# Two transformer layers on one core: earlier inputs, mask parts made on the chip, normalization and key halves on GpSimd, and another order of the projections

## The chip, the cores and the metric

The kernel runs on one core of one Trainium2 chip. The metric is the device time in microseconds, the median of the runs. A core has five engines that run side by side, each with its own queue in program order: TensorE (PE; its weight loads are shown as PEld), VectorE (DVE), ScalarE (ACT), GpSimd (POOL) and SyncE (SP), which here only issues DMAs. PE writes its results into PSUM banks; a bank comes free again once another engine has read it.

## The reference

x has 4 sequences of 2048 tokens and 256 channels. Four sublayers follow each other, each on a layer-normalized x and each added to x:

```python
x = x + _L0_attn_ref(_layernorm(x, axis=-1), ...)   # 1 head of 64, causal, biases
x = x + _L0_ffn_ref(_layernorm(x, axis=-1), ...)    # clip to fp8 e4m3, one 256x256 product, bias
x = x + _L1_attn_ref(_layernorm(x, axis=-1), ...)   # 16 heads of 16, rotary, causal
x = x + _L1_ffn_ref(_layernorm(x, axis=-1), ...)    # mix with the token before; sigmoid(r) * (relu(k)^2 Wv)
```

Everything but the fp8 product is computed in float32. `_layernorm` subtracts the mean and divides by the root of the variance plus 1e-5.

## The kernel before

**Tiling.** A block is 512 tokens of one sequence (`BLK`), four tiles of 128 (`TT`); a sequence has 4 blocks (`qb` 0 to 3), so there are 16 blocks, in the order of `order`. Because of the causal mask, block `qb` attends to `qb + 1` blocks of keys. Many helpers work on a half block (`hf`), two tiles.

**Stages of a block**, each a Python generator that emits instructions and yields a rough cost:
- first layer (list `A`): `a_in` normalizes, transposes and projects; `a_mid` computes row maxima, scores, exponentials and the weighted values; `a_out` does the output product, the next normalization to fp8 (`q8`, then float16 `q16`), the FFN product and the sum into x.
- second attention, preparation (lists `Bq` and `Q`): `b_in` normalizes and transposes; `b_project` makes q, k, v for each tile and rotates q and k with five GpSimd operations; `b_keys` splits the keys into an upper half in another float32 form (`F32R`) and a lower half, the difference, and transposes them; `b_queries` copies, transposes and splits the queries.
- second attention, main loop: 4 groups of 4 heads (`g`, NG = 4), and in a group `TT * (qb + 1)` steps (`kt`), one for each tile of keys. A step emits `scores` (L622, mask at L632), four exponentials on ScalarE (L644), the weighted values of the step before (`weighted`, L651), and, by `run_maxima`, the maxima of the group after (`maxima`, L597, mask at L605, reduction on VectorE at L610).
- end (list `E`): `end_half` does the output product, normalizes, mixes tokens (`mix`, ScalarE and VectorE), and computes the last FFN and the store.

**What sets the order.** The instructions of each of PE, ACT, DVE and POOL run in the order in which Python emitted them (a last loop ties each to the one before). The main loop adds a credit `rate_of(...)` in each step and `pull` spends it on the generators of E, Bq, Q and A, each of which advances at most once in a step where it yields a cost of zero or more. So work of the next block and of the block before is laid between the steps of the current one. `rate_of` spreads the remaining cost of each list over the steps until it is due: A and Bq by the third group, E and Q by the fourth. What isn't done by then is emitted at once by `force`: Bq before the maxima of the next block begin, in the last group of the current one; E and Q at the block's end.

**The start.** Constants first: identities and masks on GpSimd, then DMAs in SyncE's queue: the first block's x, weights, and 48 small copies (L187) that place 32-row pieces of an identity and two masks (`ident_p`, `mask_p`, `maskT_p`, used by L605 and L632) on every group of 32 partitions. VectorE prepares the fp8-clipped FFN weight (L155 to L161) and two small constants. Then the first two blocks are prepared in a loop of their own: block 0 up to its queries, block 1 (`A2`) beside it while the credit stays above a floor. The second block's x is loaded by `a_of(1)`, which stands after the copies in the program.

`normalize` (L241) is called by `normal_T` (for `a_in`, `b_in` and `end_half`) and by `a_out`; `stats` before it computes mean and variance on VectorE (L229, L230) and the power of -0.5 on GpSimd (L232, L234). The lower half of the keys is at L528, the copy of the transposed fp8 tile at L449, the edge copies that `mix` needs at L699 and L701, the sums of x on GpSimd at L437, L458 and L742, the rotation at L496 to L505, and the copy of queries at L558.

Of the kernel before, what the change touches and what calls it, by code (L numbers as in the profile page):

```python
# [22 lines left out]
P = 128  # L23
C = 256
# [18 lines left out]
def seq_kernel(  # L43
# [63 lines left out]
    def load_x(b, qb):  # L107
# [14 lines left out]
    bf_bc = load_row(bf, "bf_bc", C)  # L122


    wo0 = const.tile([D0 + 1, C + 1], F32, name="wo0")
# [12 lines left out]
    nc.vector.tensor_scalar(omu_sb, mu_sb, -1.0, 1.0, ALU.mult, ALU.add)  # L138
    cos_sb = const.tile([P, T // P, DK // 2], F32, name="cos_sb")
    nc.sync.dma_start(cos_sb, cosd)  # L140
    sin_sb = const.tile([P, T // P, DK // 2], F32, name="sin_sb")
    nc.sync.dma_start(sin_sb, sind)
    nsin_sb = const.tile([P, T // P, DK // 2], F32, name="nsin_sb")
    nc.vector.tensor_scalar_mul(nsin_sb, sin_sb, -1.0)

    wf16 = const.tile([P, CK, C], F16, name="wf16")
    wcf, wce, wcm = (
        work.tile([P, CK * C], F32, tag="w2", name=f"wc{i}", bufs=W2) for i in range(3)  # L150
    )
    nc.sync.dma_start(
        wcf.rearrange("p (k n) -> p k n", k=CK), wfT.rearrange("(k p) n -> p k n", p=P)
    )
    nc.vector.tensor_scalar(wcf, wcf, 448.0, -448.0, ALU.min, ALU.max)  # L155
    nc.vector.tensor_scalar(
        wce.bitcast(I32), wcf.bitcast(I32), 0x7F800000, None, ALU.bitwise_and
    )
    nc.vector.tensor_scalar(wcm, wce, 2.0**-6, 1.5 * 2.0**20, ALU.max, ALU.mult)
    nc.vector.tensor_tensor(wcf, wcf, wcm, ALU.add)  # L160
    nc.vector.tensor_tensor(  # L161
        wf16.rearrange("p k n -> p (k n)"), wcf, wcm, ALU.subtract
    )

# [13 lines left out]


    parts = []
    for src, name in ((ident_b, "ident_p"), (mask_b, "mask_p"), (maskT_b, "maskT_p")):
        t = const.tile([P, HG, P], BF16, name=name)
        for h in range(HG):
            for v in range(HG):
                nc.sync.dma_start(  # L187
                    t[h * SLOT : (h + 1) * SLOT, v, :], src[v * SLOT : (v + 1) * SLOT, :]
                )
        parts.append(t)  # L190
    ident_p, mask_p, maskT_p = parts

# [26 lines left out]
    def full(n, keep=2):  # L219
        return live[0] + n > W2 - keep  # L220
# [13 lines left out]
        nc.gpsimd.tensor_tensor(y, v, mhalf[:, :2], ALU.pow)  # L234
        return mv, y

    def normalize(x, hf, my, dst):

        mv, y = my
        for j in range(2):  # L240
            nc.vector.tensor_scalar(  # L241
                dst[:, j, :], x[:, 2 * hf + j, :], mv[:, j, 0:1], y[:, j : j + 1],
                ALU.subtract, ALU.mult, saturate=False,
            )
# [18 lines left out]
    def normal_T(x, out_to, hf, tag):  # L263

        my = stats(x, hf, tag)
        yield 0.0
        while full(2):
            yield None
        xn = w2n(f"xn_{tag}_{hf}")
        normalize(x, hf, my, xn)  # L270
        yield 0.0
        if not out_to:
            out_to.append(w2t(f"xT_{tag}_{hf}"))
        transpose(xn, out_to[0], f"{tag}_{hf}", nc.scalar.copy)
        done(1)
        yield 0.6
# [134 lines left out]
    def a_out(b, qb, x, hf):  # L411

        tag = f"a0_{b}_{qb}"
        while (b, qb) not in ctx0:
            yield None
        cx = ctx0[b, qb]
        t2 = slice(2 * hf, 2 * hf + 2)
        for t in range(2 * hf, 2 * hf + 2):
            o = bank(f"po_{tag}_{t}")
            nc.tensor.matmul(  # L420
                o[:, : C + 1], cx[:, t * P : (t + 1) * P], wo0, start=True, stop=True
            )
            rs = small.tile([P, 1], F32, tag="rs0", name=f"rs_{tag}_{t}")
            nc.vector.reciprocal(rs, o[:, C : C + 1])
            nc.vector.scalar_tensor_tensor(
                x[:, t, :], o[:, :C], rs, x[:, t, :], ALU.mult, ALU.add
            )
        if hf:
            done(1)
        my = stats(x, hf, f"f{tag}")  # L430
        yield 1.0

        q8 = work.tile([P, 2, C], FP8, tag="q8", name=f"q8_{tag}_{hf}", bufs=2)
        normalize(x, hf, my, q8)
        q16 = work.tile([P, 2, C], F16, tag="h16", name=f"q16_{tag}_{hf}", bufs=3)
        nc.gpsimd.tensor_copy(q16, q8)
        nc.gpsimd.tensor_tensor(  # L437
            x[:, t2, :], x[:, t2, :], bf_bc[:, None, :].to_broadcast([P, 2, C]), ALU.add
        )
        yield 0.0  # L440
        pt = bank(f"ptf_{tag}_{hf}", F16)
        for k in range(CK):
            for j in range(2):
                at = k * HALF + j * P
                nc.tensor.transpose(
                    pt[:, at : at + P], q16[:, j, k * P : (k + 1) * P], ident_h
                )
        qhT = work.tile([P, CK, HALF], F16, tag="h16", name=f"qhT_{tag}_{hf}", bufs=3)
        nc.vector.tensor_copy(qhT, pt[:, :BLK].rearrange("p (k n) -> p k n", k=CK))  # L449
        yield 0.5  # L450
        po = bank(f"pof_{tag}_{hf}")
# [66 lines left out]
    def b_keys(b, qb):  # L518

        tag = f"a1_{b}_{qb}"  # L520
        for t in range(TT):
            while (b, qb, t) not in roped or count[0] < roped[b, qb, t][0] + 2:
                yield None
            _, qk, kn = roped.pop((b, qb, t))
            kn2 = kn.rearrange("p (h z d) -> p h z d", z=2, d=DK)
            rk = qk[:, C:].rearrange("p (h d) -> p h d", d=DK)
            nc.scalar.copy(kn2[:, :, 0, :], rk)
            nc.vector.tensor_tensor(  # L528
                kn2[:, :, 1, :], rk, kn2[:, :, 0, :].bitcast(F32), ALU.subtract
            )  # L530
# [12 lines left out]
            done(1)  # L543
            flags.add((b, qb, "k", t))
            yield -0.5
# [130 lines left out]
    def end_half(b, qb, x, cn, hf):  # L676
# [22 lines left out]
            nc.gpsimd.tensor_copy(xs_[:, :, 0:1], edges.pop((b, qb - (1 - hf), 1 - hf)))  # L699
        edges[b, qb, hf] = small.tile([P, CK, 1], F32, tag="edge", name=f"edge_{tag}", bufs=3)  # L700
        nc.gpsimd.tensor_copy(edges[b, qb, hf], xs_[:, :, HALF : HALF + 1])  # L701
        while full(3) or (hf and (b, qb, "mid") not in flags):
            yield None
        mix = []
# [81 lines left out]

    def a_of(i):
        b, qb = order[i]
        if i > 0:
            xs[b, qb] = load_x(b, qb)  # L790
        x = xs[b, qb]
        a_load[0] += 13 + 9 * (qb + 1)
        return [a_out(b, qb, x, 0), a_out(b, qb, x, 1), a_mid(b, qb),
                a_in(b, qb, x, 0), a_in(b, qb, x, 1)]
# [73 lines left out]
    def rate_of(i, g, kt, n):  # L868

        to = lambda where: max(where * n - (g * n + kt), 1)  # L870
        rate = BASE
        first = a_load[0] if a_next == i + 2 else 0.0
        if first > 0 or Bq:
            rate = max(rate, first / to(1.5), (first + b_load[0] + e_load[0] / 2) / to(3))
        return max(rate, (q_load[0] + e_load[0]) / to(4))


    A.extend(a_of(0))
# [28 lines left out]
    for G, (i, b, qb, g) in enumerate(groups):  # L907
# [5 lines left out]
        for kt in range(n):  # L913
# [122 lines left out]
```

## Time and profile before

| | |
|---|---|
| runs, median (lowest to highest) | 3472.14 us (3472.14 to 3476.44), 3 runs |
| profiled execution, its own time | 3472.42 us |
| its span | 3470.6 us |
| mean granted PE clock | 0.928 |
| PE / DVE / ACT / POOL busy | 3179.8 / 2045.0 / 1801.8 / 634.7 us |
| L241 on DVE, 128x256: for `xn_a`, `q_a`, `xn_f` | x128, x64, x64: 48.6, 31.6, 30.0 us |
| L528 on DVE, 128x256 | x64, 33.9 us |
| L449 on DVE, 128x512 | x32, 12.3 us |
| L558 on POOL, copy of 128x256 | x128, 407 ns each |
| L505 on POOL, two inputs of 128x256 | x64, 730 ns each |
| L187 on SP, mask copies | x48 |

The span runs from the first instruction to the last on the core; the run's own time is a little longer. Busy time is the sum of an engine's instructions without overlap. A row of the timeline has start, time, engine, line, operation, output and inputs, shapes and count; in brackets stands how long the engine was idle before it and whose result ended that. A row of a table by stretches has, for each engine, busy us and (in brackets) the number of instructions, then the mean clock that PE was granted (1.00 is full), the share of time in which DMA engines were busy and what they moved in GB/s.

### The profile page before, as it was taken

To read this page: it belongs to the slowest core of one execution; us is meant where nothing else is said; L and a number is where in the kernel's file an instruction comes from. 1 tells how busy PE (TensorE), PEld (TensorE's weight loads), DVE (VectorE), ACT (ScalarE), POOL (GpSimd) and SP (SyncE) were. 2 spreads that over 40 slices of the span, in tenths; PEclk is the share of its full clock that TensorE was granted. 3 is DMA by queue.
4 is the path that set the end of the run, shared out by engine and by line. 5 is a ranking of instruction groups with operands and counts; after the bars stand their busy time and mean duration, and the time that the engine had idled before them with its cause. 6 is when DMAs were issued, how large, how long until landed. Compare 5 with 4: busy or idle time off the path is not lost.

```text
span 3470.6 us, 75157 instructions
## 1 busy us (share of the span) xinstructions
PE 3179.8 (92%) x31392; PEld 1736.6 (50%) x31392; DVE 2045.0 (59%) x4439; ACT 1801.8 (52%) x3678; POOL 634.7 (18%) x985
## 2 busy tenths in 40 slices
PE   3799999999998999999999899899999899989998
PEld 2455545454455554545446454444545555444444
DVE  2465656666645675576645665567663567555662
ACT  1345446455554644646555464555655454554555
POOL 1421303121112300313003220122110321021000
PEclk9899899989997999989999799998999899998899
DMA  2000000000000000000000000000000000000000
GB/s 61 1 2 14 1 2 14 1 4 10 1 2 13 14 2 1 13 1 14 2 1 8 7 14 2 4 10 1 14 2 2 13 5 5 1 7 1 7 2 7
DMA packets 22918, 24.78 MB, mean 7 GB/s; under 512 B 3953, under 2 KB 22322, under 8 KB 22578
## 3 DMA queue, kind: packets, MB, share of 16 engines
q1 hardware_dynamic: 22578, 19.97, 1.8%
q8 instruction: 247, 4.05, 0.5%
q14 instruction: 93, 0.76, 0.1%
HBM read 11.18 MB, written 8.39 MB: 6 GB/s over the span
## 4 chain that ended last, share of the span: by engine, by line
PE 71%; DVE 17%; ACT 5%; POOL 3%; issue 3%; SPq 1%; DMA 0%; POOLq 0%; ACTq 0%; DVEq 0%
PE s L622 16%; PE av L651 15%; PE m L597 11%; DVE mx L610 11%; PE av_a L398 3%; PE pq_a L258 3%; ACT p L644 2%; PE pv_a L258 2%; PE pk_f L721 2%; PE po_f L258 2%; PE s_a L386 1%; PE pw_f L258 1%; PE s L632 1%; PE pq_a L318 1%; PE pt_c L662 1%
## 5 line engine op out<-in xcount | busy, mean ns | idle before, releaser
L610 DVE TENSOR_REDUCE mx<-m 128x1 f32<-128x512 f32 (+3 forms) x2560 | 1378.8, 603 | 935.2 <-PE m L597 535.5
L644 ACT ACTIVATE p<-s 128x512 f32<-128x512 f32 (+3 forms) x2560 | 1206.2, 533 | 1009.2 <-PE s L622 517.0
L651 PE MATMUL av<-p,v_a 128*32 128x512 f32 (+3 forms) x5120 | 640.7, 572 | 0.0
L622 PE MATMUL s<-qh_a,kT_a 32*128 32x512 f32 (+3 forms) x2560 | 539.2, 475 | 60.8 <-DVE mx L610 30.2
L597 PE MATMUL m<-kT_a,qh_a 32*128 32x512 f32 (+3 forms) x2560 | 465.4, 488 | 60.2 <-ACT p L644 28.2
L597 PEld LDWEIGHTS m<-kT_a,qh_a 32*128 32x128 f32 x2560 | 207.8, 194 | 573.6 <-issue 154.0
L622 PEld LDWEIGHTS s<-qh_a,kT_a 32*128 32x128 f32 x2560 | 244.3, 189 | 412.7 <-DVE mx L610 120.4
L622 PE MATMUL s<-ql_a,kT_a 32*128 32x512 f32 (+3 forms) x2560 | 338.0, 407 | 0.0
L597 PE MATMUL m<-kT_a,ql_a 32*128 32x512 f32 (+3 forms) x2560 | 328.8, 410 | 0.0
L622 PE MATMUL s<-sh,ones 32*128 32x512 f32 (+3 forms) x2560 | 310.5, 378 | 0.0
L622 PEld LDWEIGHTS s<-sh,ones 32*128 32x128 f32 x2560 | 184.1, 194 | 18.8 <-ACT sh L292 1.6
L232 POOL TENSOR_SCALAR v_f<-mv_f 128x2 f32<-128x2 f32 x32 | 7.2, 225 | 1012.9 <-DVE mv_f L230 1012.4
L651 PEld LDWEIGHTS av<-p,v_a 128*32 128x32 f32 x5120 | 105.5, 111 | 166.4 <-issue 144.3
L597 PEld LDWEIGHTS m<-kT_a,ql_a 32*128 32x128 f32 x2560 | 163.4, 200 | 0.0
L622 PEld LDWEIGHTS s<-ql_a,kT_a 32*128 32x128 f32 x2560 | 160.8, 193 | 0.0
L398 PE MATMUL av_a<-p_a,v_a 128*65 128x512 f32 (+3 forms) x320 | 146.1, 538 | 0.5
L394 ACT ACTIVATE p_a<-s_a 128x512 f32<-128x512 f32 (+3 forms) x160 | 85.4, 534 | 100.3 <-PE s_a L389 62.4
L258 PE MATMUL pq_a<-wqkv,xT_a 128*128 128x512 f32 x256 | 124.8, 610 | 0.9 <-ACT p L644 0.9
L232 POOL TENSOR_SCALAR v_a<-mv_a 128x2 f32<-128x2 f32 x64 | 14.1, 221 | 515.2 <-DVE mv_a L230 514.3
L605 PE MATMUL m<-mask_p,ident_p 32*128 32x128 bf16 (+3 forms) x4096 | 107.3, 205 | 0.0
L632 PE MATMUL s<-maskT_p,ident_p 32*128 32x96 bf16 (+3 forms) x4096 | 105.9, 199 | 0.0
L361 DVE TENSOR_REDUCE mx_a<-m_a 128x1 f32<-128x512 f32 (+3 forms) x160 | 87.7, 603 | 17.0 <-PE m_a L360 14.0
(156 smaller groups left out, 3913.8 us busy)
## 6 DMA issues: line engine op xcount, KB each, us to landing
x<-in_x SPq DMA_DIRECT2D x16, 512.0 KB, 4.0
out_y<-x SPq DMA_DIRECT2D x32, 256.0 KB, 2.1
wqkv<-in_wqkv1T SPq DMA_DIRECT2D x1, 768.0 KB, 8.7
wqk<-in_wqk0T SPq DMA_DIRECT2D x1, 256.0 KB, 4.4
wo<-in_wo1T SPq DMA_DIRECT2D x1, 256.0 KB, 9.1
wr<-in_wrT SPq DMA_DIRECT2D x1, 256.0 KB, 9.1
wk<-in_wkT SPq DMA_DIRECT2D x1, 256.0 KB, 7.2
wv<-in_wvT SPq DMA_DIRECT2D x1, 256.0 KB, 5.8
```

The lines of the kernel that those rows point to most:

```text
L258: nc.tensor.matmul(dst, lhsT[:, k, t * P : (t + 1) * P], w[:, k, :], start=(k == 0), stop=(k == CK - 1),)
L361: nc.vector.reduce_max(mx[:, t, kb : kb + 1], sc[:, :w], axis=AX.X)
L394: nc.scalar.activation(pT[:, c0:], sc[:, c0:], AF.Exp, scale=D0**-0.5)
L398: nc.tensor.matmul(av[: D0 + 1, c:], v0[k // TT][:, k % TT, :], p[:, c:], start=(k == 0), stop=(k == nkt - 1),)
L597: nc.tensor.matmul(scs[h][:, :w], q[r, cols], kT1[b, kb][r, g, :w], start=(q is qh), stop=(kb < qb and q is ql),)
L605: nc.tensor.matmul(scs[h][:, w - P + v * SLOT : w], ident_p[r, v, :], mask_p[r, v, v * SLOT :], start=False, stop=(v == HG - 1),)
L610: nc.vector.reduce_max(mx[:, t, h, kb : kb + 1], scs[h][:, :w], axis=AX.X)
L622: nc.tensor.matmul(scs[h][:, c0:], ones[r, :] if i == 2 else kT1[b, kt // TT][r, g, kcols], sh[r, c0:] if i == 2 else (qh, ql)[i][r, c0:], ...
L632: nc.tensor.matmul(scs[h][:, c0 : c0 + (v + 1) * SLOT], ident_p[r, v, :], maskT_p[r, v, : (v + 1) * SLOT], start=False, stop=(v == HG - 1),)
L644: nc.scalar.activation(pTs[h][:, c0:], scs[h][:, c0:], AF.Exp, scale=DK**-0.5)
L651: nc.tensor.matmul(av[h * SLOT : (h + 1) * SLOT, c0:], v1[b, kt // TT][:, kt % TT, at : at + SLOT], pTs[h][:, c0:], start=(kt == 0), stop= ...
L721: nc.tensor.matmul(pk[:, d * HALF : (d + 1) * HALF], wk[:, k, d * P : (d + 1) * P], xk[:, k, :], start=(k == 0), stop=(k == CK - 1),)
```

## The change

1. **Loads.** `order[1]`'s x is loaded right after the first projection's weights; `bf`, the FFN weight, cos and sin move ahead of the second layer's weights; `a_of` loads x only from the third block on.
2. **`prepare`.** The seven VectorE instructions on the FFN weight, `nsin_sb` and `omu_sb` stand in a function that is called in the fourth round of the start loop. Their three scratch buffers count as live until then.
3. **Mask parts.** Each part is made on the first 32 partitions by a memset and a select on GpSimd, and copied to the other three groups of 32: 9 copies in place of 48.
4. **Engines.** `normal_T`'s `normalize` and the lower half of the keys run on GpSimd; the copy of the transposed fp8 tile on ScalarE. `a_out`'s `normalize` stays on VectorE.
5. **Order.** `end_half` yields once more before the mix. `rate_of` gives E more weight ahead of its due time, adds `b_load` to what is due by the fourth group, and adds a part of A beyond its next needs (`rest`). In short blocks (`n == TT`) Bq comes ahead of E. In the start loop the credit begins at 0 and `A2` may go down to -2.5.

```diff
+    xs[order[1]] = load_x(*order[1])
...
+    def prepare():
+        wcf, wce, wcm = wfs
...
+        nc.vector.tensor_scalar_mul(nsin_sb, sin_sb, -1.0)
+        nc.vector.tensor_scalar(omu_sb, mu_sb, -1.0, 1.0, ALU.mult, ALU.add)
...
-    for src, name in ((ident_b, "ident_p"), (mask_b, "mask_p"), (maskT_b, "maskT_p")):
+    for name, keep, fill, first, step in (
+        ("ident_p", ALU.not_equal, 1.0, 1, -1),
+        ("mask_p", ALU.is_ge, NEG, 1, -1),
+        ("maskT_p", ALU.is_ge, NEG, -1, 1),
+    ):
         t = const.tile([P, HG, P], BF16, name=name)
-        for h in range(HG):
-            for v in range(HG):
-                nc.sync.dma_start(
-                    t[h * SLOT : (h + 1) * SLOT, v, :], src[v * SLOT : (v + 1) * SLOT, :]
-                )
+        nc.gpsimd.memset(t[:SLOT], 0.0)
+        nc.gpsimd.affine_select(
+            out=t[:SLOT], in_=t[:SLOT], pattern=[[first * SLOT, HG], [step, P]],
+            compare_op=keep, fill=fill, base=0, channel_multiplier=first,
+        )
+        for h in range(1, HG):
+            nc.sync.dma_start(t[h * SLOT : (h + 1) * SLOT], t[:SLOT])
...
-    def normalize(x, hf, my, dst):
+    def normalize(x, hf, my, dst, engine):
         mv, y = my
         for j in range(2):
-            nc.vector.tensor_scalar(
+            engine.tensor_scalar(
...
-        normalize(x, hf, my, xn)
+        normalize(x, hf, my, xn, nc.gpsimd)
...
-        normalize(x, hf, my, q8)
+        normalize(x, hf, my, q8, nc.vector)
...
-        nc.vector.tensor_copy(qhT, pt[:, :BLK].rearrange("p (k n) -> p k n", k=CK))
+        nc.scalar.copy(qhT, pt[:, :BLK].rearrange("p (k n) -> p k n", k=CK))
...
-            nc.vector.tensor_tensor(
+            nc.gpsimd.tensor_tensor(
                 kn2[:, :, 1, :], rk, kn2[:, :, 0, :].bitcast(F32), ALU.subtract
             )
...
         nc.gpsimd.tensor_copy(edges[b, qb, hf], xs_[:, :, HALF : HALF + 1])
+        yield 0.0
         while full(3) or (hf and (b, qb, "mid") not in flags):
...
-        if i > 0:
+        if i > 1:
             xs[b, qb] = load_x(b, qb)
...
-            rate = max(rate, first / to(1.5), (first + b_load[0] + e_load[0] / 2) / to(3))
-        return max(rate, (q_load[0] + e_load[0]) / to(4))
+            rate = max(
+                rate, (first + e_load[0] / 2) / to(1.5), (first + b_load[0] + e_load[0] / 3) / to(3)
+            )
+        rest = a_load[0] - 12.0 if a_next == i + 3 else 0.0
+        rest = min(max(rest, 0.0), 1.5 * to(4))
+        return max(rate, (b_load[0] + q_load[0] + e_load[0] + rest) / to(4))
...
+    live[0] += 3
     while Bq or Q:
-        credit = 1.0
+        if count[0] == 3:
+            prepare()
+            done(3)
+        credit = 0.0
         pull([Bq, Q, A], -1e9)
-        pull([A2], -4.0 if A else -6.0)
+        pull([A2], -2.5)
...
-            pull([first, E, Bq, Q] if first else [E, Bq, Q, A], 0.0)
+            lists = [Bq, E, Q, A] if n == TT else [E, Bq, Q, A]
+            if first:
+                lists = [A] + lists[:3]
+            pull(lists, 0.0)
```

More of the change, by code (lines that the diff above doesn't have):

```diff
@@ L121, in seq_kernel @@
     bv_bc = load_row(bv0, "bv_bc", D0)
-    bf_bc = load_row(bf, "bf_bc", C)
+    xs[order[1]] = load_x(*order[1])
     wo0 = const.tile([D0 + 1, C + 1], F32, name="wo0")
@@ L129, in seq_kernel @@
     nc.sync.dma_start(wo0[D0 : D0 + 1, :C], bo0.rearrange("(o c) -> o c", o=1))
-    wqkv1 = load_w(wqkv1T, "wqkv1", 3 * C)
+    bf_bc = load_row(bf, "bf_bc", C)
+    wf16 = const.tile([P, CK, C], F16, name="wf16")
+    wfs = [work.tile([P, CK * C], F32, tag="w2", name=f"wc{i}", bufs=W2) for i in range(3)]
+    nc.sync.dma_start(
+        wfs[0].rearrange("p (k n) -> p k n", k=CK), wfT.rearrange("(k p) n -> p k n", p=P)
+    )
+    wqkv1 = load_w(wqkv1T, "wqkv1", 3 * C)
+    cos_sb = const.tile([P, T // P, DK // 2], F32, name="cos_sb")
+    nc.sync.dma_start(cos_sb, cosd)
+    sin_sb = const.tile([P, T // P, DK // 2], F32, name="sin_sb")
+    nc.sync.dma_start(sin_sb, sind)
+    nsin_sb = const.tile([P, T // P, DK // 2], F32, name="nsin_sb")
     wo1 = load_w(wo1T, "wo1", C)
@@ L137, in seq_kernel @@
     omu_sb = const.tile([P, 2, CK], F32, name="omu_sb")
[L138 to L150, printed above, removed]
-    )
-    nc.sync.dma_start(
-        wcf.rearrange("p (k n) -> p k n", k=CK), wfT.rearrange("(k p) n -> p k n", p=P)
-    )
-    nc.vector.tensor_scalar(wcf, wcf, 448.0, -448.0, ALU.min, ALU.max)
-    nc.vector.tensor_scalar(
[L157 to L160, printed above, removed]
-    nc.vector.tensor_tensor(
-        wf16.rearrange("p k n -> p (k n)"), wcf, wcm, ALU.subtract
-    )
+    def prepare():
+        wcf, wce, wcm = wfs
+        nc.vector.tensor_scalar(wcf, wcf, 448.0, -448.0, ALU.min, ALU.max)
+        nc.vector.tensor_scalar(
+            wce.bitcast(I32), wcf.bitcast(I32), 0x7F800000, None, ALU.bitwise_and
+        )
+        nc.vector.tensor_scalar(wcm, wce, 2.0**-6, 1.5 * 2.0**20, ALU.max, ALU.mult)
+        nc.vector.tensor_tensor(wcf, wcf, wcm, ALU.add)
+        nc.vector.tensor_tensor(
+            wf16.rearrange("p k n -> p (k n)"), wcf, wcm, ALU.subtract
+        )
+        nc.vector.tensor_scalar_mul(nsin_sb, sin_sb, -1.0)
+        nc.vector.tensor_scalar(omu_sb, mu_sb, -1.0, 1.0, ALU.mult, ALU.add)
     pads = []
@@ L182, in seq_kernel @@
     parts = []
-    for src, name in ((ident_b, "ident_p"), (mask_b, "mask_p"), (maskT_b, "maskT_p")):
-        t = const.tile([P, HG, P], BF16, name=name)
-        for h in range(HG):
-            for v in range(HG):
-                nc.sync.dma_start(
-                    t[h * SLOT : (h + 1) * SLOT, v, :], src[v * SLOT : (v + 1) * SLOT, :]
-                )
+    for name, keep, fill, first, step in (
[3 more added lines that the diff above has]
+    ):
+        t = const.tile([P, HG, P], BF16, name=name)
+        nc.gpsimd.memset(t[:SLOT], 0.0)
+        nc.gpsimd.affine_select(
+            out=t[:SLOT], in_=t[:SLOT], pattern=[[first * SLOT, HG], [step, P]],
+            compare_op=keep, fill=fill, base=0, channel_multiplier=first,
+        )
+        for h in range(1, HG):
+            nc.sync.dma_start(t[h * SLOT : (h + 1) * SLOT], t[:SLOT])
         parts.append(t)
@@ L235, in stats @@
         return mv, y
-    def normalize(x, hf, my, dst):
+    def normalize(x, hf, my, dst, engine):
         mv, y = my
         for j in range(2):
-            nc.vector.tensor_scalar(
+            engine.tensor_scalar(
                 dst[:, j, :], x[:, 2 * hf + j, :], mv[:, j, 0:1], y[:, j : j + 1],
@@ L527, in b_keys @@
             nc.scalar.copy(kn2[:, :, 0, :], rk)
-            nc.vector.tensor_tensor(
+            nc.gpsimd.tensor_tensor(
                 kn2[:, :, 1, :], rk, kn2[:, :, 0, :].bitcast(F32), ALU.subtract
@@ L873, in rate_of @@
         if first > 0 or Bq:
-            rate = max(rate, first / to(1.5), (first + b_load[0] + e_load[0] / 2) / to(3))
-        return max(rate, (q_load[0] + e_load[0]) / to(4))
+            rate = max(
+                rate, (first + e_load[0] / 2) / to(1.5), (first + b_load[0] + e_load[0] / 3) / to(3)
+            )
+        rest = a_load[0] - 12.0 if a_next == i + 3 else 0.0
+        rest = min(max(rest, 0.0), 1.5 * to(4))
+        return max(rate, (b_load[0] + q_load[0] + e_load[0] + rest) / to(4))
     A.extend(a_of(0))
```

## The prediction

> **What bounds the kernel now.** I read the page's engine rows and slices first, then the chain, then the stretches where TensorE (PE) is idle. The page:
>
> ```profile
> PE 3179.8 (92%) x31392; PEld 1736.6 (50%) x31392; DVE 2045.0 (59%) x4439; ACT 1801.8 (52%) x3678; POOL 634.7 (18%) x985
> ...
> PE   3799999999998999999999899899999899989998
> ...
> PEclk9899899989997999989999799998999899998899
> ...
> PE 71%; DVE 17%; ACT 5%; POOL 3%; issue 3%; SPq 1%; DMA 0%; POOLq 0%; ACTq 0%; DVEq 0%
> ```
>
> PE is the bound: 92% busy and 71% of the chain. The rest is 3470.6 - 3179.8 = 291 us of idle PE, and matmuls under a lowered clock. The first slice (3) is the emptiest. The timeline of the first 51 us says why:
>
> ```profile
> 5.50 0.90 POOL L179 MEMSET ones<- 2x128 f32 x4
> ...
> 14.67 10.07 SPq L187 DMA_DIRECT2D ident_p<-ident_b  x16
> 24.78 10.09 SPq L187 DMA_DIRECT2D mask_p<-mask_b  x16
> ...
> 45.04 1.68 SPq L109 DMA_DIRECT2D x<-in_x  x3
> 49.29 0.43 DVE L229 BATCH_NORM_STATS2 st_a<-x 128x6 f32<-128x256 f32 x1 [28.45 <-DMA x<-in_x]
> ...
> 50.82 2.56 PE L252 MATMUL pt_a<-ident,xn_a 128*128 128x128 f32 x8 [50.82 <-DVE xn_a L241]
> ```
>
> SyncE's queue issues 48 small mask transfers from 14.67 to 45.04 us, 0.63 us each, and the second block's x stands behind them. VectorE (DVE) has the first block's statistics at 20.8 us, but its next instruction is for the second block, so the first block's normalization also waits, and PE starts at 50.82.
>
> Next, busy time by stretch (columns: us, PE, PEld, DVE, ACT, POOL busy, granted clock, DMA share, GB/s):
>
> ```profile
> 50.80:103.20 52.40, 45.58 (x220) 32.42 (x221) 26.69 (x77) 15.35 (x30) 12.51 (x22) 0.97 0.02 5
> 103.20:153.80 50.60, 30.39 (x217) 20.76 (x215) 21.28 (x55) 12.20 (x24) 28.36 (x40) 0.72 0.00 1
> ...
> 1031.70:1045.30 13.60, 11.55 (x77) 7.62 (x76) 9.22 (x28) 7.40 (x17) 3.35 (x9) 0.62 0.00 0
> 1066.70:1108.40 41.70, 30.52 (x325) 20.05 (x324) 22.28 (x45) 11.76 (x28) 12.74 (x19) 0.67 0.06 20
> ...
> 1372.00:1399.00 27.00, 19.13 (x161) 11.40 (x159) 13.27 (x30) 12.39 (x25) 7.20 (x12) 0.74 0.01 2
> ...
> 3150.00:3200.00 50.00, 48.57 (x373) 22.51 (x372) 30.15 (x57) 19.64 (x37) 0.00 (x0) 0.74 0.00 1
> ```
>
> From 103 to 154 us GpSimd (POOL) leads: 28 us busy, PE idle 20 us. The loss of a stretch I take as idle PE plus busy PE x (1 - clock): 11.2 + 30.5 x 0.33 = 21 us at 1066.7, the last quarter of a short (four-tile) block, and 7.9 + 19.1 x 0.26 = 13 us at 1372. The timeline at the former:
>
> ```profile
> 1070.95 0.74 POOL L558 COPY qd_a<-qr_a 128x256 f32<-128x256 f32 x2
> ...
> 1071.64 0.62 POOL L436 CAST q_a<-q_a 128x512 f16<-128x512 fp8e4 x1
> ...
> 1072.22 1.27 POOL L437 TENSOR_TENSOR x<-x,bf_bc 128x512 f32<-128x512 f32 x1
> ...
> 1075.66 1.25 PE L575 MATMUL pt_a<-ident,qd_a 128*128 128x128 f32 x4 [7.48 <-POOL qd_a L558]
> ```
>
> Projection, keys and queries of the next block are forced into one place, and PE waits 7.48 us for POOL.
>
> **The start.** x of both blocks is now issued third and before the weights that are needed later; 48 mask transfers become 9 (39 x 0.63 = 25 us of SyncE) and nothing urgent stands behind them. POOL then decides: its preamble ended at 6.40 us and gains three memsets and three selects of 32x512. Rows: 0.20 and 0.29 us for 128x128, 0.53 for a memset of 128x512; 0.35 + 0.8 each, so 3.4 us (bounds 1.5 to 5). Then v and y of two blocks (1.0 each by the 21.02 to 22.06 rows) and two normalizations: PE starts at 6.4 + 3.4 + 2.0 + 1.0 = 12.8 us.
>
> Up to the first projection of the second stage (was 50.8 to 103.2), the new order of PE leaves four score steps (5.8 us) and the second block's output matmuls (1.9) for later: 45 us (40 to 52). The rope stage was 33.7 us (103.2 to POOL's last qd copy at 136.9), with 7 us of the second block's work ahead of it on POOL and 2.5 in its middle. Now: 4 us to the first copy, four ropes of 4.2, four key subtractions of 0.73, qd 2.8: 26.5 us. Then 16.8 us to the first score matmul as before, plus the 1.9. Sum 12.8 + 45 + 26.5 + 18.7 = 103 against 153.8: -51.
>
> Against it: DVE now holds the weight preparation and omu, which wait for wfT, sin and mu, ahead of the first ql. mu arrived at 15.9 us; x, wfT, cos and sin (0.9 MB) now precede it, at the 138 GB/s of the first 25 us some 6.5 us more, so 22 us against a need near 19; the next block's projection covers a part: +2 (0 to 5). The second block's FFN transposes and products (2 us of PE) move behind the start: +2. **Start: -47 (-35 to -55).**
>
> **Normalization and key subtraction on POOL.** 192 normalizations of 128x256 leave DVE (mean 0.437 for 128, 0.528 for 64: 78.6 us), as do 64 subtractions of 0.53 (33.9) and 32 copies of 0.416 (12.3, to ACT at its 0.59 for the same shape, 19 us on an engine 52% busy): 125 us off DVE, 6% of its work. PE's idle time put down to DVE's maxima is 30 us, so relief is 6% of that: -2 (0 to -30). On POOL no such normalization is shown: the nearest rows are a copy of 128x256 at 0.41 and a two-input operation at 0.73. With one tensor input it is nearer the copy: 0.5. So 192 x 0.5 + 64 x 0.73 = 143 us more, 635 to 778, 9 us a block. Who waits: transposes on PE behind xn; keys' transposes behind the subtraction, which stands behind the next tile's rope; and ACT, whose mix waits for the edge copies. Until now PE's waits for POOL (34.6 for qd, 13.2 for q) are 48 us for 635, 7.6%; of 143 that is **+11** (0 to 143).
>
> The Trainium skill, "GPSIMD Engine Reference", Engine selection, speaks against the move: VectorE for elementwise work, GpSimd about half as fast with two inputs, one input about line rate. The rows agree on the direction (0.73 against 0.53). If its half rate held for normalization too, 0.41 on DVE would be an estimated 0.8 here, 200 us on POOL and +15 by the same share.
>
> **The order.** In the second to fourth sequences the new order moves the next block's projection earlier by two to three steps; the eight query and eight key transposes in the last quarter of short blocks become four or none. The added yield before mix keeps ACT from standing behind the edge copies, which is the wait at 1372 (5.19 us). Losses there: 21 x 3, 13 + 13 + 11, the similar 1031.7 (2.0 + 11.6 x 0.38 = 6.4) x 3, and 7.6 x 2 at 1466.8 and 2306.4: 134 us. The same work has to go somewhere with a POOL more loaded, so I count half back: **-67** (0 to -134). In the first short block the change goes the other way: the second block's projections start four steps later, and eight query and eight key transposes now meet in its last quarter: 21 less the present loss of 9: **+12**.
>
> The Trainium skill, "TensorE: Matmul & The Clock Gate", HAM clock gate, lays the half clock to idle windows of about 3.4 us. The row at 3150 differs: 48.6 of 50 us busy and a clock of 0.74. By the rule all half clock would leave with the stalls and the order would be worth nearer 134; by the row quiet steps can be slow without one.
>
> **Sum.** -47 - 2 + 11 - 67 + 12 = -93; 3470.6 - 93 = 3377.6 span. The median of the runs is 1.5 above the span: **3379 us**.
>
> **Rivals.**
> 1. Only the start counts; stalls change their place, or the start stays and only the order helps: 3470.6 - 47 + 1.5 = 3425. For it: each stretch's PE work remains. Against: 7.48 us for one POOL queue is a bunching that the order does away with.
> 2. All stretches vanish: 134 for 67: 3312. For it: clean four-step quarters exist (20.2 us at 990.5, clock 1.00). Against: POOL's 9 us a block.
> 3. Slower: POOL becomes the late engine during projection. In four steps of a short block it has four ropes (17 us), two normalizations, y's and subtractions, some 27 us against steps of 5 to 7. It decides once more than 47 / 16 = 2.9 us a block reach PE with the order worth nothing; with half of the 143: 3470.6 - 47 + 72 + 1.5 = 3497. Against it: POOL is 22% busy on the average.
>
> **Numbers.** Forecast 0.48, first rival 0.27, second 0.15, third 0.10. Likeliest 3379, its own range 3345 to 3405. The range 3308 to 3450 takes in most of the first two rivals and leaves out the third. 0.2% (7 us) is what a measurement tells from no change: faster 0.87, within it 0.03, slower 0.10.
>
> **What will show it.** PE's first matmul at 11 to 15 us; first score matmul near 105; normalization on POOL near 0.5 us and POOL near 778; the 7.48 us wait for qd gone in the second to fourth sequences and present near the end of the first short block; mean clock above 0.928. The forecast is wrong if xn on POOL costs over 0.8 us, or if PE's waits for POOL exceed 100 us.

## The result and the profile after

The changed kernel takes **3482.49 us** (median of 20 runs, 3471.64 to 3501.3) against 3472.14 us (20 runs, 3467.97 to 3476.44): ratio **1.0030, 95% interval 1.0018 to 1.0042**. It is slower by some 10 us; 3379 had been forecast, with 3450 as the upper end. The profiled execution has a span of 3475.7 us and a granted clock of 0.918 (before 0.928).

The page of the kernel after, its engine rows:

```profile
PE 3220.0 (93%) x31392; PEld 1748.8 (50%) x31392; DVE 1940.5 (56%) x4151; ACT 1815.5 (52%) x3710; POOL 919.3 (26%) x1247
...
PE   6889899999999999999998999999999899999997
...
PEclk9889999899998989989999799998999889997899
```

Idle PE fell from 291 to 255.7 us (3475.7 - 3220.0). But the whole of that fall lies ahead of PE's first matmul, which comes at 14.0 us in place of 50.8; behind it PE is idle for 242 us (240 before), so the stalls that the order was to remove were replaced by others. And PE's busy time rose by 40 us for the same 31392 matmuls: they ran at a lower clock. And POOL went to 919 us, not to 778.

The groups of POOL by line and shape (busy, mean ns of one):

```profile
L248 POOL TENSOR_SCALAR xn_a<-x,mv_a,y_a 128x256 f32<-128x256 f32 x128 | 157.8, 1242 | 2.2
...
L248 POOL TENSOR_SCALAR xn_f<-x,mv_f,y_f 128x256 f32<-128x256 f32 x64 | 77.8, 1227 | 0.3
L565 POOL COPY qd_a<-qr_a 128x256 f32<-128x256 f32 x128 | 48.1, 413 | 52.9 <-PE av_a L405 37.3 <-PE pt_a L582 15.6
L535 POOL TENSOR_TENSOR rb_a<-qk_a,rb_a 128x256 fp32r<-128x256 f32 x64 | 47.7, 746 | 100.7 <-ACT rb_a L534 100.7
```

A normalization takes 1.23 to 1.24 us there: three times the copy of the same shape, and more than the two-input subtraction below it. PE's waits:

```profile
PE pt_f L259 <- POOL xn_f L248: 37.4, 37, 5.3
...
PE pk_a L544 <- POOL rb_a L535: 26.8, 9, 4.9
PE pt_a L259 <- POOL xn_a L248: 26.0, 13, 14.0
...
PE ptf_a L452 <- POOL q_a L443: 11.4, 11, 1.6
PE pt_a L582 <- POOL qd_a L565: 7.5, 5, 3.3
```

(total us, times, longest.) Before, PE waited 47.8 us for POOL; now 109.1 in these five lines (111 in all), of which 14.0 is the span's beginning. The qd wait is what the new order aimed at: 34.6 us became 7.5. Three new lines take its place, which had stood under DVE before (pt_f 3.5 us, pk_a 17.0, and pt_a 57.8, of which 50.8 were the span's beginning).

The timeline of the start:

```profile
4.83 0.43 DVE L236 BATCH_NORM_STATS2 st_a<-x 128x6 f32<-128x256 f32 x1 [4.83 <-DMA x<-in_x]
...
9.37 0.63 POOL L191 TENSOR_SCALAR_AFFINE_SELECT maskT_p<-maskT_p 32x512 bf16<-32x512 bf16 x1
9.98 0.23 POOL L239 TENSOR_SCALAR v_a<-mv_a 128x2 f32<-128x2 f32 x1
...
12.60 5.70 POOL L248 TENSOR_SCALAR xn_a<-x,mv_a,y_a 128x256 f32<-128x256 f32 x4
14.03 0.48 PE L259 MATMUL pt_a<-ident,xn_a 128*128 128x128 f32 x1 [14.03 <-POOL xn_a L248]
```

PE starts at 14.03 us (forecast 12.8, before 50.82): POOL's preamble ends at 10.0, and four normalizations take 5.70. The first score matmul of the main loop comes at 119.0 us, before 153.8: 34.8 us gained, where 51 had been forecast (e1 below has it at 113.0, e3 at 108.7).

By blocks, counted from one block's first score matmul to the next one's, the first sequence gives 29.5 us of that back (836.7 to 866.2), the other three 3.6, 0.0 and 6.8. In these, second blocks became 20 to 28 us longer and third blocks 17 to 21 us shorter: work moved from one to the other, as the order says, and nothing was left over.

### The profile page after: what moved, and what is told of

It reads as the page before. It is cut to its first block, busy times and chain, and to the rows that moved or that the text cites. A ratio compares the mean times of both kernels' runs of the same rounds, so it can differ in the third digit from the quotient of the medians.

```text
span 3475.7 us, 75214 instructions
## 1 busy us (share of the span) xinstructions
PE 3220.0 (93%) x31392; PEld 1748.8 (50%) x31392; DVE 1940.5 (56%) x4151; ACT 1815.5 (52%) x3710; POOL 919.3 (26%) x1247
## 5 line engine op out<-in xcount | busy, mean ns | idle before, releaser
L658 PE MATMUL av<-p,v_a 128*32 128x512 f32 (+3 forms) x5120 | 650.6, 580 | 0.0
L248 POOL TENSOR_SCALAR xn_a<-x,mv_a,y_a 128x256 f32<-128x256 f32 x128 | 157.8, 1242 | 2.2
L239 POOL TENSOR_SCALAR v_fa<-mv_fa 128x2 f32<-128x2 f32 x32 | 7.2, 226 | 404.7 <-DVE rs_a L431 371.9
L639 PE MATMUL s<-maskT_p,ident_p 32*128 32x128 bf16 (+3 forms) x4096 | 110.4, 203 | 0.0
```

Source lines behind the costliest of these rows:

```text
L239: nc.gpsimd.tensor_scalar(v, mv[:, :, 1], LN_EPS, None, ALU.add)
L248: engine.tensor_scalar(dst[:, j, :], x[:, 2 * hf + j, :], mv[:, j, 0:1], y[:, j : j + 1], ALU.subtract, ALU.mult, saturate=False,)
L639: nc.tensor.matmul(scs[h][:, c0 : c0 + (v + 1) * SLOT], ident_p[r, v, :], maskT_p[r, v, : (v + 1) * SLOT], start=False, stop=(v == HG - 1),)
L658: nc.tensor.matmul(av[h * SLOT : (h + 1) * SLOT, c0:], v1[b, kt // TT][:, kt % TT, at : at + SLOT], pTs[h][:, c0:], start=(kt == 0), stop= ...
```

## The experiments

Before was run again beside each group of experiments, with medians of 3470.31 to 3472.42 us; ratios are to these, in brackets with the 95% interval. Differences between two experiments are taken from their medians, of 4 to 12 runs each; with intervals of 3 to 7 us to either side, a difference below some 8 us isn't clear of noise. Theory N in the first four: normalization on POOL eats the gain. O: the new order costs. S: the start's gain is absorbed whatever follows. K: the keys' lower halves cost.

**e1: normalization back on DVE.**

```diff
-        normalize(x, hf, my, xn, nc.gpsimd)
+        normalize(x, hf, my, xn, nc.vector)
```

> The changed kernel with its 192 normalizations back on VectorE, all else kept. Theory N (the normalization on GpSimd, 1.23 us each in place of the 0.5 that was forecast, is what eats the gain): PE's waits for it (37.4 + 26.0 us in the trace of the changed kernel) go, so some 63 us less: 3420 (3400 to 3440). Theory O (the new order of the work costs it: more half clock in sequences two to four): 3470 to 3482. Theory S (the start's gain of 35 us is absorbed by later waits whatever engine normalizes): 3465 to 3480.

3407.21 us, ratio 0.9816 (0.9795 to 0.9837): 75 us below the changed kernel, clock 0.926. N.

**e2: the keys' lower halves back on DVE**, normalization on POOL.

```diff
-            nc.gpsimd.tensor_tensor(
+            nc.vector.tensor_tensor(
                 kn2[:, :, 1, :], rk, kn2[:, :, 0, :].bitcast(F32), ALU.subtract
             )
```

> The changed kernel with the lower halves of the keys back on VectorE, normalization left on GpSimd. Theory N: GpSimd stays late by the normalization, so only the 27 us that PE waits for the lower halves are at stake and part of them turns into waits for the normalization: 3465 (3455 to 3480). Theory K (the lower halves are the costly move): 3440 or less. Theory O: 3475 to 3485.

3461.30 us, 0.9975 (0.9965 to 0.9984): 21 us. K falls.

**e3: both back on DVE** (the two diffs together).

> The changed kernel with both moves undone; the start, the order and the copy on ScalarE stay. Theory N: 3405 (3385 to 3425), most of it already in the run with the normalization alone undone. Theory O: 3465 to 3480, since the order stays. Theory S: 3465 to 3480.

3403.02 us, 0.9801 (0.9786 to 0.9816), in N's range. Behind a DVE that normalizes, the keys cost 4 us (e1 less e3, not clear of noise) instead of 21. The same four times say that normalization on POOL costs 58 us (e2 less e3) while the keys are on DVE, and 75 when they are on POOL too: the two moves make each other dearer by some 15 us.

**e4: the kernel before with the new start alone** (loads, mask parts, `prepare`, start loop).

> The kernel before with the start alone of the change: loads, mask parts, prepare and the start loop; engines and order as before. Theory N: the 35 us that the first score matmul came earlier, a little more since the normalizations of the start are quick again: 3432 (3422 to 3442). Theory O: the same 3432. Theory S: 3465 to 3475.

3445.56 us, 0.9925 (0.9912 to 0.9937): 25 us gained: less than N and O had (3422 to 3442), more than S (3465 to 3475). The first score matmul stands at 107.9, 46 us earlier. The first block then takes 105.5 us instead of 89.6. The stretch of that block, in before and in e4 (PE, PEld, DVE, ACT, POOL busy, clock, DMA share, GB/s):

```profile
153.80:243.40 89.60, 82.91 (x1114) 51.25 (x1113) 55.16 (x136) 41.64 (x100) 24.03 (x38) 0.89 0.01 2
```

```profile
107.90:213.40 105.50, 93.71 (x1128) 59.09 (x1127) 56.24 (x140) 42.98 (x102) 30.33 (x44) 0.78 0.01 2
```

Nearly as many matmuls, but 10.8 us more busy time at a clock of 0.78, and 5 us more idle.

**e5: the changed kernel with the old order** (`rate_of`, the lists and the yield ahead of the mix).

> The changed kernel with the order of before: rate_of, the lists and the yield ahead of the mix are back, the start and the three moves between engines stay. Theory A (each part has its own price whatever the others do: start -25, order with the fp8 copy on ScalarE -42, normalization +75, keys +4 to +21): slower than the changed kernel by about 42 us, 3515 to 3530. Rival I (normalization on GpSimd is dear only because the new order bunches projections): no slower than the changed kernel, 3450 to 3485.

3511.32 us, 1.0115 (1.0102 to 1.0128): 29 us slower than the changed kernel. The order pays with POOL loaded too; rival I falls. Of A's range it falls just short.

**e6: the kernel before with the new order alone.**

```diff
-            rate = max(rate, first / to(1.5), (first + b_load[0] + e_load[0] / 2) / to(3))
-        return max(rate, (q_load[0] + e_load[0]) / to(4))
+            rate = max(
+                rate, (first + e_load[0] / 2) / to(1.5), (first + b_load[0] + e_load[0] / 3) / to(3)
+            )
+        rest = a_load[0] - 12.0 if a_next == i + 3 else 0.0
+        rest = min(max(rest, 0.0), 1.5 * to(4))
+        return max(rate, (b_load[0] + q_load[0] + e_load[0] + rest) / to(4))
...
-            pull([first, E, Bq, Q] if first else [E, Bq, Q, A], 0.0)
+            lists = [Bq, E, Q, A] if n == TT else [E, Bq, Q, A]
+            if first:
+                lists = [A] + lists[:3]
+            pull(lists, 0.0)
```

(and the `yield 0.0` of `end_half`.)

> The kernel before with the new order alone (rate_of, the lists, the yield ahead of the mix); start, engines and the fp8 copy as before. Theory A: 3472 - 42 = 3430, 3420 to 3440. Rival F (the 42 us came from the fp8 copy on ScalarE, not from the order): 3460 to 3475. Rival I (order pays only with the new start): 3450 or more.

3441.50 us, 0.9915 (0.9899 to 0.9931): 30 us. Just above A's range (3440) and below what I asks for (3450): F falls, and I as it was put. The order pays alone, if less than together with the new start (e10).

**e7: the kernel before with normalization on POOL alone** (e1's edit the other way round, in the old kernel).

> The kernel before with the normalization of 192 tiles on GpSimd alone; start, order, keys and the fp8 copy as before. Theory A: 3472 + 75 = 3547, 3535 to 3560, with 1.23 us for each. Rival I (dear only in the new order): 3475 to 3510. My prediction's price (+11) would give 3483.

3562.53 us, 1.0263 (1.0249 to 1.0276): 91 us slower, more than A. The move is dear in the old order too, so I falls, and with it the thought that the new order's bunching makes it dear.

**e8: load without a path.** e3, and the same normalization a second time on POOL, into a buffer that nobody reads.

```diff
         normalize(x, hf, my, xn, nc.vector)
+        spare = w2n(f"spare_{tag}_{hf}")
+        normalize(x, hf, my, spare, nc.gpsimd)
+        done(1)
```

> The changed kernel with normalization and keys on VectorE, and the same normalization made a second time on GpSimd into a buffer that nobody reads: GpSimd carries its 236 us, but no transpose waits for it. Theory L (what costs is the way of x through GpSimd: transposes stand behind a 1.23 us instruction and its place in the queue): 3403 + up to 15, 3400 to 3420. Rival Q (what costs is the room taken in GpSimd's queue, so that rotations, query copies and edge copies come late): 3455 to 3485. Between them both count.

3427.07 us, 0.9872 (0.9860 to 0.9885): 24 us above e3, while POOL carries all of it:

```profile
L248 POOL TENSOR_SCALAR spare_a<-x,mv_a,y_a 128x256 f32<-128x256 f32 x128 | 161.7, 1272 | 2.2
...
L248 POOL TENSOR_SCALAR spare_f<-x,mv_f,y_f 128x256 f32<-128x256 f32 x64 | 79.0, 1244 | 0.3
```

So 24 us come from the room that 241 us take in POOL's queue (10%). The keys are on DVE here, so the price to compare is e2 less e3, 58 us: the other 34 come from PE standing behind these instructions (51 of the 75 where the keys are on POOL too, if the load costs the same there, which wasn't run). Nearer L than Q, but both count.

**e9: the disputed price by itself.** e3 with 28 instructions on scratch data ahead of the start. Its one run, 3429.40 us, holds these too and says nothing of the change.

```diff
+    for i in range(4):
+        nc.gpsimd.tensor_scalar(
+            dst[:, :C], src[:, :C], pw[:, 0:1], pw[:, 1:2], sub, mul, saturate=False
+        )
+    for i in range(4):
+        nc.gpsimd.tensor_scalar(dst[:, :C], src[:, :C], pw[:, 0:1], None, sub)
...
```

> The changed kernel with normalization and keys on VectorE, and ahead of the start 28 GpSimd instructions on scratch data, four of each: 128x256 float32 with two operations and two per-partition scalars (the form of normalization); one operation and one per-partition scalar; two operations with two constants; one operation with one constant; a copy; a two-input subtraction; and the first form on 128x512. Known from the traces: first form 1.23, copy 0.41, two inputs 0.73. Theory P1 (operations are what costs): one operation about 0.6 to 0.8 with scalar or constant, two about 1.2 with either. Theory P2 (reading per-partition scalars costs): with constants 0.4 to 0.6 for one operation and for two. Theory P3 (a fixed cost of the form): 128x512 well under twice 1.23, say 1.5 to 1.8, and all forms with scalars near 1.2. The time itself says nothing here.

The groups of POOL in its first 60 us (in the order of the expectation these are L208, L212, L214, L216, L218, L220, L222):

```profile
L222 POOL TENSOR_SCALAR wc<-wc,mhalf 128x512 f32<-128x512 f32 x4 | 8.3, 2074 | 0.4
L208 POOL TENSOR_SCALAR wc<-wc,mhalf 128x256 f32<-128x256 f32 x4 | 4.9, 1226 | 0.4
L214 POOL TENSOR_SCALAR wc<-wc 128x256 f32<-128x256 f32 x4 | 4.3, 1072 | 0.3
L212 POOL TENSOR_SCALAR wc<-wc,mhalf 128x256 f32<-128x256 f32 x4 | 3.7, 924 | 0.4
L216 POOL TENSOR_SCALAR wc<-wc 128x256 f32<-128x256 f32 x4 | 3.4, 851 | 0.3
L220 POOL TENSOR_TENSOR wc<-wc 128x256 f32<-128x256 f32 x4 | 2.9, 724 | 0.3
...
L218 POOL COPY wc<-wc 128x256 f32<-128x256 f32 x4 | 1.6, 402 | 0.2
```

None of the three theories holds as put. The second operation costs 0.22 (0.851 to 1.072) to 0.30 us, the per-partition scalars 0.07 to 0.15 us. But the plainest form, one operation with a constant, already takes 0.85, above the two-input subtraction's 0.72 and twice the copy. Doubling the width adds 0.85 (2.074 - 1.226); if time grows evenly with the width, an estimated 0.38 of 1.23 is there whatever the width.

**e10: e3 with the fp8 copy on DVE too**: start and order alone are left.

```diff
-        nc.scalar.copy(qhT, pt[:, :BLK].rearrange("p (k n) -> p k n", k=CK))
+        nc.vector.tensor_copy(qhT, pt[:, :BLK].rearrange("p (k n) -> p k n", k=CK))
```

> The changed kernel with normalization, keys and also the copy of the transposed fp8 tile on VectorE: start and order alone are left of the change. Theory C (the copy on ScalarE is worth nothing, start and order gain more together than apart): 3398 to 3408, as with the copy on ScalarE (3403). Rival F (start -25 and order -30 add up, and the copy on ScalarE gave the 14 us between their sum and 3403): 3412 to 3422.

**3394.74 us**, 0.9781 (0.9769 to 0.9794), the lowest median of all kernels here: below C and F both. With the copy on ScalarE it was 8 us more (e3), but the two intervals overlap (0.9786 to 0.9816 for e3), and PE's waits put down to the copy are 3.0 us in e3 and 1.2 here: a price of the copy isn't shown.

**e11: a step between normalization and transposes**, in the changed kernel.

```diff
         normalize(x, hf, my, xn, nc.gpsimd)
         yield 0.0
+        yield 0.0
```

> The changed kernel with one more yield between normalization and its transposes, so that these come one main-loop step later. Theory L (of normalization's 75 us, some 50 are transposes waiting for GpSimd's 1.23 us instructions and their queue; load alone gave 24): 3430 to 3465. Rival R (the later transposes only push the projections behind them together; the step is no longer than the queue): 3475 to 3495.

3460.19 us (3438.79 to 3470.38), 0.9962 (0.9946 to 0.9977): 22 us below the changed kernel, within L's range, near its end. PE's wait for xn_f nearly goes, others stay or grow:

```profile
PE pk_a L545 <- POOL rb_a L536: 28.7, 14, 4.9
...
PE ptf_a L453 <- POOL q_a L444: 19.4, 15, 2.0
PE pt_a L259 <- POOL xn_a L248: 19.4, 4, 16.5
PE pt_a L583 <- POOL qd_a L566: 18.0, 15, 3.3
...
PE pt_f L259 <- POOL xn_f L248: 7.0, 4, 5.3
```

**e12: e10 with the start loop's credit and floors as before** (1.0; -4 and -6).

> The changed kernel with normalization, keys and the fp8 copy on VectorE (3395), and the start loop's credit (1.0) and floors (-4 and -6) as before, so that more of the second block's work lies in the start again. Theory M (that work has to go somewhere: what the start gains by putting it off, the first short block gives back): 3388 to 3402, the first score matmul 8 to 20 us later than 109.8 and the first block as much shorter than 102.7. Rival D (putting it off pays): 3403 to 3415.

3397.17 us, 0.9786 (0.9771 to 0.9802). M, though the shift of the first score matmul, from 109.8 to 116.7, is just under its 8 us; the first block goes from 102.7 to 93.0 us. Putting the second block's work off gained nothing that can be told from noise.

**e13: only xn_f on POOL** (64 of 192; keys on DVE).

```diff
-        normalize(x, hf, my, xn, nc.gpsimd)
+        normalize(x, hf, my, xn, nc.gpsimd if tag[0] == "f" else nc.vector)
```

> The changed kernel with keys on VectorE and only the 64 normalizations ahead of the last FFN (xn_f) on GpSimd; the 128 of the two attention inputs (xn_a) are on VectorE. By the count (64 of 192, and the start's 10 us belong to xn_a): 3403 + 22 = 3425, 3418 to 3432. By the waits of the changed kernel (xn_f 37 us of PE's waits, xn_a 26): 3403 + 40 = 3443, 3435 to 3455.

3464.08 us, 0.9975 (0.9964 to 0.9985): 61 us above e3, beyond both expectations, and no less than e2, which has all 192 on POOL (3461.30). The timeline of POOL, where the second block of the second sequence has its projections:

```profile
1106.96 1.28 POOL L508 TENSOR_TENSOR qk_a<-qk_a,cos_sb 128x512 f32<-128x512 f32 x1
1108.32 0.72 POOL L511 TENSOR_TENSOR qk_a<-qk_a,rb_a 128x256 f32<-128x256 f32 x1
1109.00 0.72 POOL L512 TENSOR_TENSOR qr_a<-qk_a,rb_a 128x256 f32<-128x256 f32 x1
1109.71 4.85 POOL L248 TENSOR_SCALAR xn_f<-x,mv_f,y_f 128x256 f32<-128x256 f32 x4
```

and of PE:

```profile
1111.00 0.47 PE L259 MATMUL pt_f<-ident,xn_f 128*128 128x128 f32 x1 [2.63 <-POOL xn_f L248]
1112.21 0.90 PE L259 MATMUL pt_f<-ident,xn_f 128*128 128x128 f32 x3 [0.74 <-POOL xn_f L248]
...
1114.62 0.90 PE L259 MATMUL pt_f<-ident,xn_f 128*128 128x128 f32 x3 [0.73 <-POOL xn_f L248]
1115.31 3.62 PE L265 MATMUL pq_a<-wqkv,xT_a 128*128 128x512 f32 x4
```

Here all four tiles of a block's end come at once, behind a rotation of the next block. PE waits 2.63 us for the first and then again for each next one. The projection after it takes 3.62 us; in e3 the same four matmuls take 1.88. By stretches of 7 us (and one of 1 us), e13, then the same place in e3:

```profile
1104.00:1111.00 7.00, 3.98 (x69) 2.40 (x67) 4.88 (x9) 2.18 (x6) 6.84 (x9) 0.96 0.01 2
1110.00:1111.00 1.00, 0.00 (x1) 0.01 (x1) 0.96 (x3) 0.00 (x0) 1.00 (x2) 0.71 0.00 0
1111.00:1118.00 7.00, 5.23 (x12) 2.57 (x12) 1.09 (x4) 1.48 (x3) 3.56 (x3) 0.50 0.00 0
```

```profile
1109.60:1116.60 7.00, 5.92 (x82) 3.58 (x81) 6.97 (x12) 3.60 (x9) 6.39 (x9) 1.00 0.01 2
1116.60:1123.60 7.00, 7.00 (x79) 3.95 (x83) 5.45 (x12) 3.91 (x10) 3.99 (x5) 1.00 0.00 0
```

The stalled PE falls to a clock of 0.50: 12 matmuls in 7 us where e3 has 79 (which are smaller on the average). In the whole run e13 has 28.6 us more idle PE than e3 (3462.6 - 3225.0 against 3404.0 - 3195.0) and 30.0 us more busy PE (3225.0 against 3195.0). Each us of waiting cost about another us in clock here.

Such a place isn't the rule. POOL's 64 xn_f stand in 21 places of its queue, of which seven are right behind a rotation; of the 49 places with xn_a in the changed kernel, two are. The six blocks with those seven places make 40 of the 59 us between the two profiles, and the three blocks where xn_f stands behind the sum of x at L444 make 16. No run moved xn_f ahead of the rotation, so what the rotation itself costs is read from the traces alone.

**e14: only xn_a on POOL** (128 of 192; keys on DVE).

```diff
-        normalize(x, hf, my, xn, nc.gpsimd)
+        normalize(x, hf, my, xn, nc.gpsimd if tag[0] == "a" else nc.vector)
```

> The changed kernel with keys on VectorE and only the 128 normalizations of the two attention inputs (xn_a) on GpSimd; the 64 ahead of the last FFN are on VectorE. If the two kinds add up (75 for all, 61 for xn_f): 3403 + 14 = 3417, 3408 to 3427, of which 10 us are the start. Rival W (cost follows the count: 128 of 192): 3445 to 3460.

3415.49 us, 0.9843 (0.9830 to 0.9856): 12 us above e3, 8 of them by the first score matmul (116.7 against 108.7). The sum holds, W falls: two thirds of the instructions cost little. But the sum came out by luck: its 75 was measured with the keys on POOL. With the keys on DVE, as here, all 192 cost 58 (e2), so the parts, 61 and 12, make 15 more than the whole: with xn_f on POOL, moving xn_a too cost nothing more.

PE's waits for both, in e3, e13 and e14:

```profile
PE pt_f L259 <- DVE xn_f L248: 8.0, 11, 3.5
PE pt_a L259 <- DVE xn_a L248: 14.4, 2, 11.5
```

```profile
PE pt_f L259 <- POOL xn_f L248: 41.5, 35, 5.3
```

```profile
PE pt_a L259 <- POOL xn_a L248: 28.6, 17, 14.0
```

xn_f adds 33.5 us of waits, xn_a 14.2, and the clock differs: beside 28.6 us more idle PE, e13 has 30.0 us more busy PE, but e14, with 11.6 more idle, has 3.8 less busy (3191.2 against 3195.0). e8's 20.6 us more idle come with the same busy PE, too (3194.5). So a wait doesn't always cost its length again.

**e15: e10 with a step between normalization and transposes**, on DVE.

> The changed kernel with normalization, keys and the fp8 copy on VectorE (3395) and one more yield between normalization and its transposes. Theory L (PE still waits 10 us for xn_f on VectorE, and a step more hides it): 3378 to 3390. Rival R (the transposes only meet other work a step later): 3391 to 3410.

3431.31 us, 0.9880 (0.9865 to 0.9895): 37 us slower than e10. R in its direction, but beyond its range; the loss is spread over nearly all blocks from the first sequence's fourth on (up to 6.5 us a block), PE's busy time grows by 21.1 us (3186.6 to 3207.7), and its waits for the key split from 6.8 to 13.5 us and for qd from 10.5 to 17.3. Why it is so much wasn't settled.

## Why the prediction was wrong

The runs form a ladder from before to after, one part at a time:

| step | from, to (us) | measured | forecast |
|---|---|---|---|
| start (e4) | 3472.1, 3445.6 | -27 | -47 and +12 = -35 |
| order (e10 less e4) | 3445.6, 3394.7 | -51 | -67 |
| fp8 copy to ScalarE (e3 less e10) | 3394.7, 3403.0 | +8 (hardly clear of noise) | hidden |
| keys to POOL (e1 less e3) | 3403.0, 3407.2 | +4 (not clear of noise) | in the +11 |
| normalization to POOL (after less e1) | 3407.2, 3482.5 | **+75** | +11 |
| sum | 3472.1, 3482.5 | +10 | -93 |

(DVE's relief of -2 has no step of its own; the forecast has the +12 under the order, but e4, without the new order, shows it. Prices depend on the order of the steps: order alone gave -30, normalization between +58 and +91, keys between +4 and +21.)

**The step that failed** is the one on POOL: "With one tensor input it is nearer the copy: 0.5", and "PE's waits for POOL ... are 48 us for 635, 7.6%; of 143 that is +11". It had two errors. The price: 1.23, not 0.5, so POOL took 285 us more and not 143 (634.7 to 919.3). With the right price the same share would still have given only 22, where the two moves together measured 79 (after less e3). The share was the larger error. The term's own bounds, 0 to 143, had room for the 79; the range of the whole forecast had not. 7.6% is what the average us on POOL costs; e8's 10% shows that it is about right for work that PE doesn't wait for. Normalization is not such work. Every one of its results goes straight into PE's transposes one step later. Its two kinds differ by what stands ahead of them in POOL's queue: xn_f meets the next block's rotation, some 4 us, in seven of its 21 places, +61 for 78 us on POOL; xn_a in two of 49, and it costs 12 for 158. That the price goes by kind and not by count is shown by e13 and e14; that the rotation makes the difference is argued from the traces.

**What was not in the sum at all** is the clock after a wait. I counted half clock among the losses that the order would remove, and priced a new wait at its length alone. e13 shows the length doubled; e8 and e14 show that it need not be. From e1 to the changed kernel PE has 39.5 us more idle and 30.9 us more busy time (216.2 to 255.7, 3189.1 to 3220.0).

The Trainium skill, "TensorE: Matmul & The Clock Gate", Part 1: The HAM clock gate, has the clock halve after an idle window of about 3.4 us. Here the clock fell within the wait of 2.63 us, as the 0.71 of the stretch from 1110 to 1111 us shows, and stayed at 0.50 in the next 7 us, in which PE was busy for 5.23: a wait shorter than that window was enough in this place.

The same skill's "GPSIMD Engine Reference", 4.1 Engine selection, calls GpSimd about half as fast with two inputs and roughly line rate with one. The runs here have two inputs at 0.72 to 0.75 against 0.50 to 0.53 on DVE, and one-input normalization at 1.23 against 0.41 to 0.44 for xn_a: worse with one input than with two. The 0.8 that I worked out from it was nearer than my 0.5, and still too low.

**The start** was right in its mechanism: mask copies and loads stood in SP's queue, PE starts at 14.03 us (at 11.5 in e3, where DVE normalizes), and e4's first score matmul came 46 us earlier. What I had as +12 for the first short block was +16 in e4, and the rest of the distance to -27 lies in small differences of later blocks. e12 shows what most of these are: with the old floors the first block is 10 us shorter (93.0) and the score matmul comes 7 us later, to about the same total. In the changed kernel, POOL adds its own late share at the start: keys' transposes wait 3.84 and 4.79 us there for the subtraction behind the next rotation. The forecast named this queue, but priced it at 0.73 an instruction.

**The order** was right as forecast, -51 of -67, and the 7.48 us wait for qd has gone from the second to fourth sequences. But alone it gave -30; start and order together gave 76 against the before run beside them, 20 more than apart. Why they help each other wasn't settled.

**The fp8 copy** was taken as hidden on an engine 52% busy. The 8 us between e10 and e3 are hardly clear of noise, so whether it was hidden stays open.

**The third rival** had the right mechanism (POOL late in the projections) and a fair size (72 for the measured 79 of both moves), but I gave it 0.10 and tied it to an order worth nothing. Its counter-argument, "POOL is 22% busy on the average", was the fault: e8 shows that busy share isn't what decides. Both signs that I had set for being wrong came: 1.23 us where 0.8 was the limit, and PE's waits for POOL above 100.

## What to carry to other kernels

Before an operation moves to an idle engine, look who reads its result and how soon: 158 us of it cost 12 here, and 78 us elsewhere cost 61. A new wait of TensorE can cost twice its length where the clock falls with it (e13), or its length alone (e8, e14). Measure the form itself on the new engine: my 0.5, taken from the nearest row by number of inputs, was off by a factor of 2.5. Start and order without the engine moves make 3394.7 us, 2.2% below before.

## What the runs showed of the hardware

- GpSimd's tensor-scalar form costs 0.85 us for 128x256 float32 with one constant, twice its copy (0.40), and more than a two-input subtraction (0.72).
- From run to run of one kernel, time goes with the granted clock: e11's 12 runs go from a span of 3437.0 us at a clock of 0.929 to 3468.6 at 0.917.
- A normalization ahead of the last FFN takes 0.70 us on DVE in e10 (64, 697 ns), while the same shape for the attention inputs takes 0.42 (128, 416 ns). The trace shows what slows it. All 34 of the 64 that took longer than 0.5 us (0.65 to 1.44) ended 0.15 us after the end of a GpSimd instruction that had begun before them or within 0.01 us of their start; the other 30 took 0.38 to 0.42 us. So DVE stood still until GpSimd's instruction was done. Four in a row, and GpSimd's rotation beside them:

```profile
703.52 3.24 DVE L248 TENSOR_SCALAR xn_f<-x,mv_f,y_f 128x256 f32<-128x256 f32 x4
```

```profile
703.80 0.73 POOL L503 TENSOR_TENSOR rb_a<-qk_a,nsin_sb 128x256 f32<-128x256 f32 x1 [2.65 <-ACT qk_a L497]
704.49 0.77 POOL L503 TENSOR_TENSOR rb_a<-qk_a,sin_sb 128x256 f32<-128x256 f32 x1
705.34 1.27 POOL L508 TENSOR_TENSOR qk_a<-qk_a,cos_sb 128x512 f32<-128x512 f32 x1
```
